# New times for VectorE, GpSimd and row-group visits in the planner that writes a decoder layer's order of issue

## The chip, the core and the metric

The kernel runs on one core of a Trainium2 chip. The core has TensorE (PE in the profile: matrix products into PSUM, eight banks), VectorE (DVE), ScalarE (ACT), GpSimd (POOL) and SyncE (SP, whose queue here starts all transfers). Each engine works through its own list of instructions in order and waits at semaphores for the others. The metric is device time in microseconds, from one launch, lower is better.

## The reference

One post-norm decoder layer on eight sequences of 256 tokens with 256 channels, in float32:

```
x = layernorm(x + attn(x))              # three attentions, 16 heads of 96, mixed by a gate
x = layernorm(x + cross(x, ctx, mask))  # 16 heads of 16 over 256 context tokens
x = layernorm(x + moe(x))               # 8 experts 256->1024->256, all computed, weights of the top 2 router scores
```

The first attention is the sum of three softmaxes with one query: keys from a latent of 32 columns (causal), keys from the 64 tokens with the highest importance score, and plain causal keys. Weights of the expert part: `softmax(one_hot(top2) * scores)`; since the softmax runs over all eight experts, none of them is left out.

## The kernel before, in words

The kernel is written as Python generators ("threads"), one for each kind of work: `project` (queries and keys of a group of four heads), `first` (scores), `weighing` (softmax), `parking` (probabilities are transposed in blocks on VectorE and written to DRAM), `products` (read back from DRAM, probabilities times values), `between` (output projection, first layernorm), `second`, `x_weighing`, `x_products` (cross attention), `after` (second layernorm, router), `experts`, `finish` (third layernorm, store), and loaders. A sequence `s` has four head groups `g`. For the first sequence (`s` = 0) the probabilities are turned by TensorE (`pt`) and copied from PSUM, for the others they go through DRAM (lines 648 to 695).

No loop sets the order in which instructions stand in the engines' lists. A small planner does, `Machine` (from line 131). A thread yields its next operation as an `Op` with a cost in microseconds. `Machine.start` (line 203) works out when it could begin: its engine free, its inputs written, a buffer free. `Machine.run` (line 248) commits, again and again, the operation that could start earliest, and within 0.1 us of it the one of the lowest rank; the rank is a number of the thread's stage and of four times the sequence. So **the costs decide the order**, and the order is all that they decide: no instruction is added or dropped by them, but they also choose the engine where a thread yields a pair. `copied` (line 329) yields VectorE or ScalarE for a copy, `experts` yields either for the ReLU `h`, and `weighing` yields VectorE or GpSimd for one subtraction; the planner takes the one that it believes ends first.

The costs stand in `dve_us` (line 109), `act_us` (line 119), `pool_us` (line 125), in `mm` (line 308: `2 * 0.00084` us for each column, divided by `share` where four products run side by side in TensorE's row or column groups), and in `group` (line 323), which packs several products into one operation and adds `extra` us. Line 100 of the profile is the place where every VectorE, ScalarE and GpSimd instruction is issued, line 315 every product, line 321 every transpose on TensorE, line 306 every transfer: groups are told apart by tile names.

Names that the prediction uses, all as in the profile: `s` are scores of the first attention, with source `kx` for plain and selected keys (probabilities `pr`) and `lx`, `kn` for the latent keys (probabilities `pl`); `o` their product with the values; `pyo` an output projection; `ptx` the transposed, normalised rows; `xpq`, `xq` the cross attention's query; `sx` its scores, `nmx` their negated maxima, `prx` its probabilities, `ox` its products; `pi`, `ppos`, `psel` the choice of the 64 tokens; `plg`, `prt` the router; `ph`, `h`, `py` an expert's two products and the ReLU. "(1,0)" is sequence 1, group 0.

The experts have rank 99: their products (945 of the 1581 us that TensorE is busy) fill whatever the other threads leave open. They need the second layernorm's output of their own sequence, so **there is no filler before the first sequence has passed both attentions**: the first `ph` starts at 236.75 us. PSUM has eight banks for all of this, of which the threads other than `experts` may hold six from then on; SBUF buffers of probabilities are three, shared by `pr`, `pl` and `prx`.

Of the kernel before, what the change touches and what calls it, by code (L numbers as in the profile page):

```python
# [15 lines left out]
PSUM = bass.MemoryType.PSUM  # L16
# [37 lines left out]
def free_size(ap):  # L54
    return math.prod(ap.shape[1:])
# [29 lines left out]
class Issuer:  # L85
# [5 lines left out]
    def __getattr__(self, kind):  # L91
        def make(*args, **kw):
            given = list(args) + list(kw.values())
            aps = [x for x in given if isinstance(x, bass.AP)]
            outs = [kw["out"]] if "out" in kw else [args[0]]
            if kw.get("accum_out") is not None:
                outs.append(kw["accum_out"])
            ins = [x for x in aps if all(x is not y for y in outs)]
            us = self.cost(kind, max(free_size(x) for x in aps), kw)
            return Op(self.name, us, outs, ins, lambda: getattr(self.engine, kind)(*args, **kw), lag=LAG[self.name])  # L100

        return make
# [3 lines left out]
LAG = {"DVE": 0.08, "ACT": 0.1, "POOL": 0.04}  # L106


def dve_us(kind, n, kw):
    if kind == "reciprocal":  # L110
        return 0.06 + 0.0063 * n
    if kind in ("bn_stats", "bn_aggr"):
        return 0.34 if kind == "bn_stats" else 0.1
    if kind in ("match_replace", "max"):
        return 0.42 if n > 8 else 0.2
    return 0.07 + 0.00105 * n + {"scalar_tensor_tensor": 0.06, "tensor_tensor": 0.05}.get(kind, 0.0)


def act_us(kind, n, kw):
    if kind == "copy":  # L120
        return 0.06 + 0.00083 * n
    return 0.16 + 0.00083 * n + (0.1 if kw.get("accum_out") is not None else 0.0)


def pool_us(kind, n, kw):
    if kind == "tensor_tensor":
        return {2: 0.7, 4: 1.0}.get(n, 0.2 + 0.00163 * n)
    return {"tensor_scalar": 0.25 + 0.0025 * n}.get(kind, 0.13 + 0.0009 * n)


class Machine:
# [162 lines left out]
def decoder_layer(ctx: ExitStack, tc: tile.TileContext, a: dict, out: bass.AP):  # L294
    nc = tc.nc
    ctx.enter_context(tc.manual_schedule(engines=ENGINES))
    m = Machine()
    V = Issuer("DVE", nc.vector, dve_us)
    A = Issuer("ACT", nc.scalar, act_us)
    G = Issuer("POOL", nc.gpsimd, pool_us)  # L300

    def dma(out, in_, queue="SP"):
        engine = {"SP": nc.sync, "ACT": nc.scalar}[queue]
        on_chip = out if out.space in ON_CHIP else in_
        size = math.prod(on_chip.shape) * (1 if on_chip.dtype == U8 else 4)
        return Op(queue, 0.6, [out], [in_], lambda: engine.dma_start(out=out, in_=in_), size=size)

    def mm(out, lhsT, rhs, start=True, stop=True, share=1):
        us = 2 * 0.00084 * max(free_size(rhs), free_size(lhsT)) / share
        return Op(  # L310
            "PE",
            us,
            [out],
            [lhsT, rhs],
            lambda: nc.tensor.matmul(out, lhsT, rhs, start=start, stop=stop, skip_group_check=share > 1),  # L315
            lag=0.17,
        )
# [5 lines left out]
    def group(ops, extra=0.0):  # L323
        op = Op("PE", sum(o.us for o in ops) + extra, [], [], lambda: [o.issue() for o in ops], lag=0.17)
        op.writes = list(dict.fromkeys(k for o in ops for k in o.writes))
        op.reads = list(dict.fromkeys(k for o in ops for k in o.reads))
        return op

    def copied(dst, src):

        return V.tensor_copy(dst, src), A.copy(dst, src)
# [13 lines left out]
    def mtile(shape, name):  # L345
        return mtile_(shape, "m", name)
# [9 lines left out]
    def seen(*key):  # L356
        return lambda: (key if len(key) > 1 else key[0]) in done
# [631 lines left out]
    def latent_heads(name):  # L989

        for s in range(B):
            yield 2 + AHEAD * s
            d = pro.setdefault(s, {})
            yield seen("heads", s, 0)
            lk = d["lk"]
            t = (one if name == "kn" else two)([P, NHG, T], name, name)
            ps = [mtile([P, T], "p" + name) for _ in range(NHG)]
            yield m.claim(t)
            yield m.claim(*ps)
            ops = []  # L1000
            for i in range(1 if name == "kn" else 2):
                for g, p_ in enumerate(ps):
                    rows = bass.ts(g, 32)
                    if name == "kn":
                        ops.append((p_, wkv[rows, 0], lk[rows]))
                    else:
                        ops.append((p_[:, bass.ts(i, P)], lk[rows, bass.ts(i, P)], wkv[rows, 1]))
            yield group([mm(*op, share=4) for op in ops], 0.1)
            for g, p_ in enumerate(ps):
                yield copied(t[:, g], p_)  # L1010
                m.release(p_)
            d[name] = t
            done.add((name, s))
            if name != "kn":
                yield seen("kn", s)
                m.release(lk)


    def scores(h, d, g, st, which):


        spans = ((0, N0), (N0, N0 + P)) if which == 0 else ((0, P), (P, T))
        ops = []
        for qt, (lo, n) in enumerate(spans):
            for i in range(3):
                for j in range(HG):
                    rows = bass.ts(j, 32)
                    if which == 0:
                        key = h["kx"][rows, i, 0:n]
                    else:  # L1030
                        key = d["kn"][rows, g, 0:n] if i == 2 else d["lx"][rows, i, 0:n]
                    ops.append(
                        mm(st[j][:, lo : lo + n], h["q"][rows, i, bass.ts(qt, P)], key, i == 0, i == 2, share=4)
                    )
        return group(ops, 0.1)

    def first():
        for s in range(B):
            yield 2 + AHEAD * s
            d = pro.setdefault(s, {})  # L1040
            for g in range(NHG):
                yield seen("heads", s, g)
                h = heads[s, g]
                for which, name in enumerate(("pr", "pl")):
# [6 lines left out]
                    st = [mtile([P, 2 * T], "s") for _ in range(HG)]  # L1051
                    yield m.claim(*st)
                    yield scores(h, d, g, st, which)
                    if which:
                        m.release(h["q"])
# [149 lines left out]
    def kept_in_dram(shape, name):  # L1205
        d = dram.tile(shape, F32, tag=name, name=name)
        Op.kept.add(d.tensor.name)
        return d

    def slots(d, x):  # L1210

        for j in range(HG):
            yield dma(x[bass.ds(32 * j, XH)].rearrange("p g t -> p (g t)"), d.rearrange("(j d i) x -> j d (i x)", j=HG, i=2)[j])
# [62 lines left out]
    def second():  # L1276
        for s in range(B):
            yield 1 + AHEAD * s
            yield seen("middle", s)
            yield seen("query weights")  # L1280
            d, xT, xr = xa.setdefault(s, {}), xTs[s], xrs[s]

            pq = mtile([P, 2, T], "xpq")
            for i in range(2):
                yield group([mm(pq[:, i], xWq[:, k, bass.ts(i, P)], xT[:, k, :], k == 0, k == 1) for k in range(2)])
            qc = one([P, 2, T], "side", "qc")
            for i in range(2):
                yield (
                    A.activation(qc[:, i], pq[:, i], AF.Identity, bias=qb[:, i : i + 1], scale=0.25),
                    V.tensor_scalar(qc[:, i], pq[:, i], 0.25, qb[:, i : i + 1], ALU.mult, ALU.add),  # L1290
                )
            m.release(pq)
            dq = kept_in_dram([P, 2 * T], f"cq{s % 2}")
            yield dma(dq, qc.rearrange("p i t -> p (i t)"))
            m.release(qc)
            yield from slots(dq, xq)
            for i in range(2):
                yield G.tensor_tensor(xr[:, i, :], xr[:, i, :], bo, ALU.add)
            done.add(("bias", s))
            yield seen("context", s)  # L1300
            for g in range(NHG):
                pr = three([P, HG * 2 * T], "p", "prx")
                yield m.claim(pr)
                if g:
                    yield seen("read x", s, g - 1)
                st = [mtile([P, 2, T], "sx") for _ in range(HG)]
                yield m.claim(*st)
                yield group(
                    [
                        mm(st[j][:, qt], xq[bass.ts(j, 32), g, bass.ts(qt, P)], xk[bass.ts(j, 32), g, :], share=4)  # L1310
                        for qt in range(2)
                        for j in range(4)
                    ],
                    0.1,
                )
                d[g] = {"pr": pr, "st": st}
                done.add(("prx", s, g))
# [312 lines left out]
```

## Time and profile before

| what | us |
|---|---|
| three runs: median (lowest, highest) | 1637.23 (1637.2, 1640.49) |
| the profiled execution's own time | 1636.81 |
| its span, first to last instruction | 1635.1 |
| TensorE busy (share of the span) | 1580.7 (97%) |
| VectorE, ScalarE, GpSimd busy | 1101.8 (67%), 592.9 (36%), 612.1 (37%) |
| mean granted TensorE clock | 0.991 |

The profile page has each engine's busy time, the span in 40 slices, the chain that ended last, and the costliest groups of instructions. Other views of the same execution give waits (which engine waited, at which tile, for whom), stretches (busy time and granted clock in a window) and a timeline. TensorE's matmul records overlap, since a product's record covers its pipeline; what a stream of products costs is read from one start to the next.

### The profile page before, as it was taken

The numbers are of one execution on the slowest core, as the hardware profiler recorded it, in microseconds if no ns is written. First come the engines' busy times: TensorE is split into PE (matmuls) and PEld (weight loads), VectorE is DVE, ScalarE is ACT, GpSimd is POOL, SyncE is SP. The second block draws the span as 40 slices with busy tenths as digits, with TensorE's granted clock in tenths as the row PEclk, the third lists the DMA queues.
The fourth block names the chain that finished last, engine by engine and source line by source line (L and its number), as shares of the span: only waits on it lengthen the run. The fifth ranks groups of instructions, "written<-read, shape, count | busy, mean of one in ns | idle before, by whom it ended". The sixth has DMA issues, their size and how long they took to land.

```text
span 1635.1 us, 31737 instructions
## 1 busy us (share of the span) xinstructions
PE 1580.7 (97%) x12028; PEld 1302.6 (80%) x12028; DVE 1101.8 (67%) x2359; ACT 592.9 (36%) x2185; POOL 612.1 (37%) x820
## 2 busy tenths in 40 slices
PE   7889789999999999999999999999999999999998
PEld 6767568887787788788887778878888788888887
DVE  4775687778978755888777854667768683644333
ACT  2564553454453331444355412234435440400000
POOL 4754735354445421444344521334435430310000
PEclk9999899999999999999999999999999999999999
DMA  6511426668766794757658774945747895674553
GB/s 191 152 45 47 164 92 221 198 212 280 230 203 235 236 329 135 273 174 245 206 182 288 253 256 130 325 119 193 246 162 242 276 325 182 219 251 143 160 155 97
DMA packets 185769, 329.95 MB, mean 202 GB/s; under 512 B 13313, under 2 KB 105617, under 8 KB 178449
## 3 DMA queue, kind: packets, MB, share of 16 engines
q1 hardware_dynamic: 185616, 327.92, 60.6%
q8 instruction: 96, 1.57, 0.4%
q14 instruction: 57, 0.46, 0.1%
HBM read 237.70 MB, written 90.19 MB: 201 GB/s over the span
## 4 chain that ended last, share of the span: by engine, by line
PE 74%; issue 7%; DVE 6%; POOL 1%; DMA 1%; ACT 0%; POOLq 0%; DVEq 0%; SPq 0%; ACTq 0%
PE py L315 22%; PE ph L315 22%; PE s L315 7%; PE o L315 3%; PE pk L315 2%; PE pyo L315 2%; PE sx L315 2%; PE ox L315 2%; PE pv L315 1%; PE pkm L315 1%; PE pq L315 1%; PE pks L315 1%; DVE pl L100 1%; DVE pr L100 1%; PE xpq L315 1%
## 5 line engine op out<-in xcount | busy, mean ns | idle before, releaser
L315 PE MATMUL ph<-xT,w 128*128 128x256 f32 x2048 | 476.9, 382 | 0.7 <-DVE turn L100 0.4
L315 PE MATMUL py<-w,h 128*128 128x256 f32 x2048 | 467.8, 381 | 0.0
L315 PEld LDWEIGHTS ph<-xT,w 128*128 128x128 f32 x2048 | 383.0, 190 | 66.3 <-issue 12.1
L315 PEld LDWEIGHTS py<-w,h 128*128 128x128 f32 x2048 | 385.0, 190 | 58.8 <-issue 6.7
L100 DVE TENSOR_SCALAR h<-ph,b 128x256 f32<-128x256 f32 x329 | 158.8, 483 | 133.2 <-PE ph L315 131.3
L100 ACT ACTIVATE h<-ph,b 128x256 f32<-128x256 f32 x183 | 86.6, 473 | 279.5 <-PE ph L315 273.4
L100 DVE SCALAR_TENSOR_TENSOR xr<-py,rw,xr 128x256 f32<-128x256 f32 x128 | 61.5, 480 | 170.5 <-PE py L315 169.6
L100 POOL TENSOR_TENSOR prx<-prx,sumsx 128x512 f32<-128x512 f32 x128 | 129.9, 1046 | 95.5 <-DVE sumsx L100 46.7
L100 POOL TENSOR_TENSOR rstd<-var,nhalf 128x2 f32<-128x2 f32 x24 | 17.3, 722 | 356.7 <-DVE var L100 356.4
L100 ACT ACTIVATE prx<-sx,nmx 128x256 f32<-128x256 f32 x256 | 117.7, 486 | 53.5 <-DVE nmx L100 42.7
L100 POOL TENSOR_TENSOR kx<-turn 128x64 f32<-128x64 f32 (+1 forms) x128 | 65.5, 530 | 178.8 <-DVE turn L100 171.5
L100 POOL TENSOR_TENSOR pr<-pr,wpr 128x256 f32<-128x256 f32 (+2 forms) x128 | 130.5, 1050 | 0.0
L100 ACT ACTIVATE pl<-pl,nmpl 128x128 f32<-128x128 f32 (+1 forms) x256 | 113.6, 448 | 18.9 <-DVE nmpl L100 18.7
L100 ACT ACTIVATE pr<-pr,nmpr 128x128 f32<-128x128 f32 (+1 forms) x256 | 113.7, 447 | 0.0
L100 DVE TENSOR_TENSOR pr<-s,causal 128x256 f32<-128x256 f32 x128 | 74.8, 584 | 38.2 <-PE s L315 34.4
L100 POOL TENSOR_TENSOR pl<-pl,wpl 128x512 f32<-128x512 f32 x64 | 93.0, 1467 | 2.0
L315 PE MATMUL s<-kx,q 32*128 32x192 f32 (+1 forms) x1536 | 92.5, 383 | 0.9 <-POOL kx L100 0.9
L100 POOL TENSOR_TENSOR q<-turn 128x256 f32<-128x256 f32 x64 | 45.5, 728 | 123.3 <-DVE turn L100 123.3
L100 DVE TENSOR_TENSOR pl<-s,causal 128x256 f32<-128x256 f32 x128 | 74.6, 583 | 15.4 <-PE s L315 13.0
L100 DVE TENSOR_REDUCE nmx<-sx 128x2 f32<-128x512 f32 x128 | 79.1, 680 | 7.2 <-PE sx L315 7.2
L315 PEld LDWEIGHTS s<-kx,q 32*128 32x128 f32 x1536 | 68.1, 185 | 18.4 <-issue 6.5
L100 DVE TENSOR_REDUCE nmpr<-pr 128x4 f32<-128x256 f32 (+2 forms) x128 | 80.0, 676 | 0.0
(220 smaller groups left out, 2300.5 us busy)
## 6 DMA issues: line engine op xcount, KB each, us to landing
w<-in_W SPq DMA_DIRECT2D x256, 512.0 KB
pr<-pr SPq DMA_DIRECT2D x28, 1024.0 KB
pa<-pr SPq DMA_DIRECT2D x28, 1024.0 KB
prx<-prx SPq DMA_DIRECT2D x28, 1024.0 KB
xpt<-prx SPq DMA_DIRECT2D x28, 1024.0 KB
pl<-pl SPq DMA_DIRECT2D x28, 768.0 KB
pb<-pl SPq DMA_DIRECT2D x28, 768.0 KB
xT<-in_xT SPq DMA_DIRECT2D x8, 256.0 KB
```

The costliest lines, as they stand in the source:

```text
L100: return Op(self.name, us, outs, ins, lambda: getattr(self.engine, kind)(*args, **kw), lag=LAG[self.name])
L315: lambda: nc.tensor.matmul(out, lhsT, rhs, start=start, stop=stop, skip_group_check=share > 1),
```

## The change

Only the planner's costs change. The functions that make them get a new argument: whether an operand lies in PSUM.

- VectorE: `bn_stats` 0.34 to 0.43 us, `bn_aggr` 0.1 to 0.15; every other operation costs at least 0.11; an operation with `accum_out` (a sum on the side) costs 0.14 more; the additions of 0.06 and 0.05 for `scalar_tensor_tensor` and `tensor_tensor` go, and instead an operation with 256 elements and a PSUM operand costs 0.18 more (`tensor_tensor`) or 0.06 more (`scalar_tensor_tensor`, `tensor_scalar`). Plain copies keep their cost. For the ReLU of 128x256 elements that is 0.339 to 0.399 us on VectorE, beside 0.372 us (unchanged) on ScalarE.
- GpSimd: `tensor_tensor` with 4, 256 and 512 elements 1.0 to 0.87, 0.617 to 0.68 and 1.03 to 1.0 us; `tensor_scalar` by a hundredth or so.
- TensorE: the extra for a visit of row groups (`s`, `sx`, `pkn`, `pvl`) 0.1 to 0.4 us.

```diff
-            us = self.cost(kind, max(free_size(x) for x in aps), kw)
+            us = self.cost(kind, max(free_size(x) for x in aps), kw, any(x.space == PSUM for x in aps))
...
-def dve_us(kind, n, kw):
+def dve_us(kind, n, kw, psum):
     if kind == "reciprocal":
         return 0.06 + 0.0063 * n
     if kind in ("bn_stats", "bn_aggr"):
-        return 0.34 if kind == "bn_stats" else 0.1
-    if kind in ("match_replace", "max"):
-        return 0.42 if n > 8 else 0.2
-    return 0.07 + 0.00105 * n + {"scalar_tensor_tensor": 0.06, "tensor_tensor": 0.05}.get(kind, 0.0)
+        return 0.43 if kind == "bn_stats" else 0.15
+    if kind in ("max", "max_index"):
+        return 0.2
+    us = max(0.07 + 0.00105 * n, 0.11)
+    if kw.get("accum_out") is not None:
+        return us + 0.14
+    if psum and n == 256:
+        return us + {"tensor_tensor": 0.18, "scalar_tensor_tensor": 0.06, "tensor_scalar": 0.06}.get(kind, 0.0)
+    return us
...
     if kind == "tensor_tensor":
-        return {2: 0.7, 4: 1.0}.get(n, 0.2 + 0.00163 * n)
-    return {"tensor_scalar": 0.25 + 0.0025 * n}.get(kind, 0.13 + 0.0009 * n)
+        return {2: 0.7, 4: 0.87, 256: 0.68, 512: 1.0}.get(n, 0.2 + 0.00163 * n)
+    return {"tensor_scalar": 0.26 + 0.0024 * n}.get(kind, 0.13 + 0.0009 * n)
...
-            yield group([mm(*op, share=4) for op in ops], 0.1)
+            yield group([mm(*op, share=4) for op in ops], 0.4)
...
-        return group(ops, 0.1)
+        return group(ops, 0.4)
...
-                    0.1,
+                    0.4,
```

## The prediction

> **What bounds the kernel now.** I read the page's busy times first, then the stretches, then the waits of TensorE before and after 250 us, then the timeline where the longest waits stand.
>
> ```profile
> PE 1580.7 (97%) x12028; PEld 1302.6 (80%) x12028; DVE 1101.8 (67%) x2359; ACT 592.9 (36%) x2185; POOL 612.1 (37%) x820
> ...
> 0.00:50.00 50.00, 39.19 (x307) 32.17 (x308) 26.33 (x76) 14.80 (x46) 25.50 (x57) 1.00 0.66 191
> ...
> 150.00:200.00 50.00, 38.77 (x292) 30.76 (x292) 34.86 (x62) 28.85 (x115) 35.90 (x46) 0.86 0.41 142
> ...
> 250.00:1500.00 1250.00, 1242.17 (x9462) 1021.35 (x9461) 887.18 (x1832) 468.75 (x1744) 462.50 (x602) 1.00 0.68 227
> 1500.00:1600.00 100.00, 100.00 (x465) 88.04 (x464) 35.50 (x77) 0.47 (x1) 0.69 (x1) 1.00 0.50 151
> ```
>
> The columns of a stretch are its length, then busy time and instructions of PE, PE's weight loads, DVE, ACT and POOL, then TensorE's granted clock, DMA share and GB/s. From 250 to 1500 us TensorE idles 7.8 of 1250 us and runs at full clock: its own work is the limit there. In the first 250 us it is busy 210 us (39.2 + 45.3 + 42.1 + 38.8 + 44.9 over the five fifties), idle 40, and the clock falls to 0.86 in one fifty. So a new order can save at most what the start loses, and the few us of waits that come later.
>
> The waits of TensorE up to 250 us (sum, times, longest), and those behind 250 us after the line of dots:
>
> ```profile
> PE pt L321 <- POOL pr L100: 6.3, 5, 1.8
> PE pl L315 <- DMA wA<-in_w_krope: 5.6, 1, 5.6
> PE ppos L315 <- DVE gm L100: 5.5, 3, 2.1
> PE o L315 <- DVE nmx L100: 4.8, 1, 4.8
> PE sx L315 <- ACT prx L100: 4.7, 1, 4.7
> PE ptx L321 <- DVE xr L100: 2.4, 1, 2.4
> ...
> PE prt L321 <- DVE rw L100: 2.1, 1, 2.1
> PE ptx L321 <- DVE xr L100: 1.3, 2, 1.0
> ```
>
> All those of the start sum to 39.8 us, those behind it to 7.6. The two longest stand side by side:
>
> ```profile
> 182.25 2.07 PE L315 MATMUL sx<-xk,xq 32*128 32x256 f32 x10 [4.74 <-ACT prx L100]
> 189.09 1.51 PE L315 MATMUL o<-pa,vw 128*32 128x256 f32 x16 [4.77 <-DVE nmx L100]
> ...
> 181.13 0.23 DVE L100 RECIPROCAL wpr<-wpr 128x16 f32<-128x16 f32 x1
> 186.08 2.31 DVE L100 STREAM_TRANSPOSE pr<-pr 128x2048 f32<-128x2048 f32 x1 [4.71 <-POOL pr L100]
> 188.39 1.83 DVE L100 TENSOR_REDUCE nmx<-sx 128x2 f32<-128x512 f32 x3
> ```
>
> The reader is to see a queue blocked at its head: a transpose of `pr` stands on VectorE right behind the reciprocal that GpSimd's weighting of the same `pr` needs; VectorE idles 4.71 us for GpSimd, and the maxima `nmx` of the next `sx` wait behind it.
>
> **How I count.** No instruction is added or dropped, so I price TensorE's list and compare lists. From start to start in this trace: a product over 256 columns 0.432 us (two records of 0.215; 465 records in 100 us of the end), over 128 columns 0.223, a transpose 0.11, a product in row or column groups a quarter, and 0.1 more at each change between full array and groups (0.309 us instead of 0.216 for the record before it). The order of issue has 321 such changes before and 321 after: TensorE's own work is the same, 1529.7 us by these prices in both lists. What changes is the time lost beside it. I call "loss" the traced start of a group less the prices of all that stands ahead of it. Before: 16.3 us at the first scores, 25.7 at `o` (0,0), 37.0 at (0,3), 39.3 at the first `sx`, 53.5 at `o` (1,0), 62.9 at the first `ph` (236.75 less 173.8), 97.2 at the last `o`. The last 34 us of that come at a rate of 3 us per 100 and are mostly what my prices leave out, as waits are 7.6.
>
> **The change part by part.**
>
> *VectorE's costs.* The masking additions `pr<-s,causal` and `pl<-s,causal` (256 of them) take 0.584 and 0.583 us by their rows; planned 0.389 before, 0.519 after. ReLUs on VectorE take 0.483, planned 0.339, now 0.399. Counting by `accum_out` takes 0.405 (128 columns) and an accumulator read of 0.08; planned 0.204, now 0.344. So the plan's VectorE lagged by about 1.0 us more per head group than it will (8 additions x 0.13), 8 us over the eight groups of the start. Against it: `xr<-pyo` takes 0.420, planned 0.389 and now 0.519. What it does to the list: **17.1 us more of TensorE's work (projections and scores of sequence 1, context products) stand ahead of the first `ph`**, 190.9 us instead of 173.8. That is filler where TensorE waits before the change.
>
> *GpSimd's costs* follow their rows more closely (256 elements 0.73 and 0.62 us, 512 elements 1.046); they move the subtraction `pr<-pr,nmpr` by four from GpSimd (31 to 27) to VectorE, 4 x 0.53 us over the whole run: nothing.
>
> *Row groups, 0.1 to 0.4.* 64 visits `s`, 32 `sx`, 16 `pkn` and `pvl`. In the timeline the 16 records of `sx` take 1.07 us to the next start (planned 0.96, now 1.26), the 24 products of one `s` 2.69 (2.68, now 2.98). The old charge was the nearer one, so this part makes the plan believe TensorE late by some 0.2 x 27 visits = 5 us in the start. A late TensorE in the plan means consumers put too early: it takes back part of the gain.
>
> *Where it lands, step by step.* (1) Up to the first `pt` (0,0) the list is nearly the same, with the same 38.4 us ahead of it; `xpv` now stands ahead of `ppos`, which moves that wait of 1.9 to `pt`. Loss 24.5 there in both: nothing gained. (2) To `o` (0,3). From `s` (kx) to its `pt` the chain needed 28.4 to 31.9 us where `pt` waited; the work in between was 32.4, 27.4 and 22.0 us for groups 1, 2, 3, and is now 27.2, 29.3 and 27.1. Group 3, 8 us short before (the waits of 1.84 and 1.38 on `pr`), is 3 short. With the 24.5 and some 2 of `ppos` the loss at `o` (0,3) becomes about 30 instead of 37: 7 gained. (3) The cross attention's query needs about 7.5 us from `xpq` (ends 153.6) to `xq` (store issued at 154.65, its read 2.56 later, the last of four reads at 158.5 and as long to land; SP's queue held nothing ahead); 7.9 us of work stand there now (16.9 before): no wait, or one of 1. (4) The four `sx`, 1.9, 2.0 and 6.3 us apart before, stand 7.0, 8.9 and 9.8 apart. Eight exponentials take 8 x 0.705 = 5.6 us, so the bank waits of 4.74, 0.76 and 0.53 go. On VectorE 3.7 us of work (`nmpl`, `turn` and others) now stand between that reciprocal and the transpose; but on GpSimd the four weightings of `prx` (4.03 us) have moved in between those of `pr`, so GpSimd needs 0.6 + 2.95 + 4.03 + 1.25 = 8.8 us: VectorE again waits some 5 us, and what queues behind it is the second `nmx`, the copies out of PSUM, and so the third `sx`. I leave 4 us for it, and 3 to 4 for `o` (1,0), whose read-back from DRAM comes 3 us late. (5) `o` (1,1) moves up from 178.2 to 152.9 us of work, with 23.6 us from its `s` (lx) instead of 26.9, where unstalled groups of later sequences had no less than 33.2: it waits, up to 10 us less what (4) already took, some 5. Loss at that point 30 + 2.5 + 8 + 5 = 45 to 47. (6) From there to `ph`, `ox`, `ptx` and `plg` wait as before (6 us; `pyo` to `ptx` has 2.6 us of cover, 2.8 before). Loss at the first `ph` about 53 instead of 62.9: 10 us gained.
>
> *ReLUs move to ScalarE* (329 on VectorE and 183 on ScalarE become 56 and 456). A ReLU takes 0.473 there against 0.483, and both engines have room from 250 us on (ScalarE 469 of 1250 busy, plus 273 x 0.473 = 129): nothing on TensorE's path while PSUM banks come free in time. The tail from 1600 us, `py` to the last store, is the same list: nothing.
>
> **A rule beside the row.** The granted clock was 0.86 between 150 and 200 us, and the 48 `o` products at 189.09 took 3.4 us to the next group, against 1.87 at 131.95; the losses above hold this already. The Trainium skill, "TensorE: Matmul & The Clock Gate", Part 1, says that an idle window of about 3.4 us brings the clock to half. By it, my waits of step 4, each near that length, may or may not cost 1.5 us each again; the sum would be 8 to 11 us instead of 10.
>
> **The sum.** 1635.1 - 10 = 1625.1 us of span, + 1.7 around it (1636.81 less 1635.1) = 1626.8, + 0.4 (the median stands that much above the profiled run): 1627.
>
> **The rivals.**
> - *The chain does not get longer at all* (0.12). First `ph` stays at 236.75; then all 17.1 us are gained: 1620. For it: the waits of the start exceed that. Against: steps 4 and 5.
> - *VectorE paces the start* (0.14). The rows' times of what stands ahead of the second layernorm's `var` on VectorE sum to 186 us against 177; if the start stretches with that, `ph` is at 236.75 x 186/177 = 248.8, 5 us gained: 1632. For it: the blocked queue. Against: VectorE is busy 156 of 235 us there.
> - *Waits only change place* (0.12): the loss stays 62.9, the blocked transpose being paid in full at `sx` and `o` (1,1): 1637.
> - *ScalarE's queue turns into the bound of the middle: slower* (0.25). A ReLU at the head of ScalarE's list waits for its `ph` (279.5 us of idle before 183 of them, 1.5 each), and exponentials stand behind it, so `sx` and `s` banks come free later. 456 x 2.0 us of ReLUs and waits and the 382 us of other work of 250 to 1500 pass 1250. Price: one bank wait like the 4.74; from the third on (14.2 us) it eats the gain and the measurement's bound; one in each of the seven later sequences is 33 - 10 = 23 us slower, 1660. Against it: ReLU waits are there because ScalarE has nothing better, and the planner gives a reader of PSUM the first rank.
>
> **How the numbers follow.** My forecast has 0.37, the two other gains 0.12 and 0.14: faster by over 0.2% (3.3 us, what a measurement here can tell) 0.63; within 0.12; slower 0.25. The range goes from a full gain and 3 us of later waits (1617) to a ScalarE queue that costs four or five such waits (4 x 4.74 - 10 = 9 us, 1645). The likeliest case alone: 1622 to 1631.
>
> **What would show it.** The first `ph` at 240 to 247 us; no wait of `sx` on `prx` near 4.7, but one at `o` (1,0) or (1,1); waits up to 250 us near 30; PE still idle under 10 us from 250 to 1500. It is wrong if TensorE's waits after 250 us exceed 15 us, or the first `ph` comes past 254.

## The result, and the profile after

| | before | after |
|---|---|---|
| median, us (lowest to highest) | 1637.23 (1635.45 to 1644.09) | 1647.99 (1645.06 to 1650.07) |
| ratio, 95% interval | | **1.0059 (1.0042 to 1.0076)** |
| span of the profiled execution, us | 1635.1 | 1645.7 |
| first `ph` starts, us | 236.75 | 262.56 |
| TensorE work ahead of it, by the prices of the prediction, us | 173.8 | 190.9 |
| loss there (start less work), us | 62.9 | 71.7 |

The change made the kernel about 10 us slower, where 10 us of gain were forecast, and its first `ph` came past 254 us, which the prediction had named as a sign that it is wrong. The lines of the page and of the stretches that answer those of before:

```profile
PE 1585.1 (96%) x12028; PEld 1306.3 (79%) x12028; DVE 988.1 (60%) x2070; ACT 722.6 (44%) x2478; POOL 609.1 (37%) x816
...
0.00:50.00 50.00, 37.38 (x290) 30.28 (x294) 25.18 (x71) 13.40 (x36) 23.50 (x56) 1.00 0.75 223
50.00:100.00 50.00, 43.04 (x442) 35.79 (x440) 35.45 (x92) 31.09 (x116) 36.14 (x48) 0.90 0.26 80
...
150.00:200.00 50.00, 43.76 (x329) 35.18 (x327) 36.79 (x68) 25.55 (x101) 33.08 (x43) 0.90 0.35 128
200.00:250.00 50.00, 40.77 (x422) 30.91 (x422) 34.83 (x72) 26.35 (x89) 23.44 (x29) 0.93 0.30 106
250.00:1500.00 1250.00, 1236.37 (x9432) 1016.31 (x9429) 807.71 (x1645) 561.70 (x1970) 464.30 (x604) 1.00 0.66 225
```

ReLUs have gone from VectorE (1101.8 to 988.1 us) to ScalarE (592.9 to 722.6), as planned. In the first 250 us TensorE is busy 210 us, as before: its 40 us of idle time are still 40. From 250 to 1500 us it idles 13.6 us instead of 7.8. TensorE's waits up to 250 us, and those behind 250 us after the dots:

```profile
PE pt L326 <- POOL pr L100: 6.6, 5, 3.4
PE pl L320 <- DMA wA<-in_w_krope: 5.7, 1, 5.7
PE ppos L320 <- DVE gm L100: 5.6, 3, 2.5
PE sx L320 <- ACT q L100: 3.6, 1, 3.6
PE o L320 <- DMA pa<-pr: 3.5, 1, 3.5
PE pks L320 <- DVE pl L100: 2.5, 1, 2.5
...
PE ptx L326 <- DVE xr L100: 4.8, 3, 2.6
PE prt L326 <- DVE rw L100: 4.4, 3, 2.1
```

The wait of `sx` on `prx` (4.74) and that of `o` on `nmx` (4.77) are gone. In their place stand waits at `sx` (3.6), `o` (3.5) and `pks` (2.5), and the sum is 40 us again.

Where the 10.6 us of span arise is seen if the time is read against the work done by then. The table has the time less the prices of all records that TensorE had started (0.1 us per change between full array and groups included; priced by the record, so it lies 2 to 4 us below the losses by the list), in us, for the two kernels and for three that come below:

| up to, us | 100 | 150 | 200 | 237 | 262 | 300 | 1600 |
|---|---|---|---|---|---|---|---|
| before | 25.2 | 35.9 | 53.0 | 61.3 | 62.1 | 64.9 | 97.6 |
| after | 30.0 | 36.8 | 50.0 | 62.4 | 68.3 | 71.9 | 108.4 |
| after, two heads of queue cleared | 28.2 | 35.0 | 49.8 | 56.8 | 64.4 | 65.7 | 99.1 |
| before, VectorE's lag 0.081 | 24.0 | 36.0 | 53.9 | 62.2 | 63.8 | 66.6 | 93.2 |
| before, VectorE's lag 0.082 | 24.4 | 32.4 | 53.8 | 63.1 | 73.1 | 78.2 | 112.8 |

Up to 237 us the two kernels have lost the same. Then the kernel before has its experts' products and stops losing; the kernel after has 17 us of moved work to do first and loses at the old pace, a quarter of a microsecond per microsecond, for 26 us more. So 7.0 of the 10.8 us arise up to 300 us, and 3.8 behind.

Two places of the timeline after show what the moved work does there. The first is around the first `sx`:

```profile
172.17 0.75 POOL L100 TENSOR_TENSOR kx<-turn 128x256 f32<-128x256 f32 x1
172.86 1.42 POOL L100 TENSOR_TENSOR xr<-xr,bo 128x256 f32<-128x256 f32 x2
173.18 2.40 DVE L100 TENSOR_TENSOR pr<-pr,nmpr 128x256 f32<-128x256 f32 x1
...
175.68 0.63 ACT L100 ACTIVATE pr<-pr 128x512 f32<-128x512 f32 x1 [9.49 <-DVE pr L100]
176.62 3.06 PE L320 MATMUL sx<-xk,xq 32*128 32x256 f32 x14 [3.58 <-ACT q L100]
```

A subtraction on VectorE takes 2.40 us here; its shortest takes 0.37. It stands beside GpSimd's additions. ScalarE's queue is blocked at its head by that `pr`, and `sx` waits for a bank that ScalarE has to empty behind it (`q`). The second place is around `o` (1,1):

```profile
211.99 1.51 PE L320 MATMUL o<-pa,vw 128*32 128x256 f32 x16 [3.47 <-DMA pa<-pr]
212.61 0.47 ACT L100 ACTIVATE kc<-xpk,xb 128x256 f32<-128x256 f32 x1 [2.46 <-DMA cv<-vc]
...
215.75 0.20 DVE L100 RECIPROCAL sumsx<-sumsx 128x8 f32<-128x8 f32 x1 [6.05 <-ACT prx L100]
215.87 5.11 DVE L100 TENSOR_TENSOR rows<-lat,ttab 128x128 f32<-128x128 f32 x2
...
215.84 0.98 POOL L100 TENSOR_SCALAR keep<-keep 1x256 f32<-1x256 f32 x1
216.81 4.02 POOL L100 TENSOR_TENSOR prx<-prx,sumsx 128x512 f32<-128x512 f32 x4
```

`kc` and `keep` are keys and their mask for sequence 1's cross attention. `kc` stands at the head of ScalarE's queue, waiting for a buffer whose content is still being stored, with five exponentials `prx` of sequence 0 behind it; GpSimd then does `kc` and `keep` first and weights `prx` at 216.81. At the same time TensorE waits for the read-back of `o` (1,1).

### The profile page after: what moved, and what is told of

Read it like the earlier page. It is cut to its first block, busy times and chain, and to the rows that moved or that the text cites. A ratio compares the mean times of both kernels' runs of the same rounds, so it can differ in the third digit from the quotient of the medians.

```text
span 1645.7 us, 31890 instructions
## 1 busy us (share of the span) xinstructions
PE 1585.1 (96%) x12028; PEld 1306.3 (79%) x12028; DVE 988.1 (60%) x2070; ACT 722.6 (44%) x2478; POOL 609.1 (37%) x816
## 4 chain that ended last, share of the span: by engine, by line
PE 81%; issue 7%; DVE 4%; DMA 4%; POOL 2%; ACT 1%; SPq 1%; POOLq 0%; DVEq 0%; ACTq 0%
PE ph L320 23%; PE py L320 22%; PE s L320 9%; PE o L320 4%; PE pk L320 3%; PE pyo L320 2%; PE sx L320 2%; PE pv L320 2%; PE ox L320 2%; PE pq L320 2%; PE pkm L320 1%; PE pks L320 1%; DMA xpt<-prx 1%; PE pt L326 1%; DVE pr L100 1%
## 5 line engine op out<-in xcount | busy, mean ns | idle before, releaser
L100 ACT ACTIVATE h<-ph,b 128x256 f32<-128x256 f32 x456 | 215.9, 473 | 415.5 <-PE ph L320 414.1
L100 DVE STREAM_TRANSPOSE prx<-prx 128x2048 f32<-128x2048 f32 x28 | 64.5, 2303 | 20.5 <-POOL prx L100 20.5
```

## Experiments

The first theory (**A**) was that the loss lies in the new order up to the second layernorm of sequence 0; its rival, that the ReLUs on ScalarE slow the middle. Letters in the expectations belong to the runs of their own group.

**Start and rest apart.** The planner changes costs when the second layernorm of sequence 0 has been planned.

```diff
+PLAN = {"new": True}                      # e2: False
+    if not PLAN["new"]:
+        return old_dve_us(kind, n, kw)    # likewise POOL and the visits
 ...
             done.add(("normed", s))
+            PLAN["new"] = False           # e2: True
```

New start, old rest:

> The changed costs are used until the first sequence has passed its second layernorm, the old ones from then on; up to the first ph the order of issue is that of the changed kernel. Theory A (the loss is in the start: first ph at 262.6 us with 190.9 us of work ahead, 71.7 lost, against 62.9 before): 8.8 us slower than before, 1646 (1644 to 1648). Theory B (ScalarE's ReLUs slow the middle): 1637 to 1639.

Old start, new rest:

> The old costs until the first sequence has passed its second layernorm, the changed ones from then on. Theory A: the first ph at 236.7 us as before, and what the changed kernel lost after its first ph, 10.7 less 8.8 = 1.9 us: 1639 (1637 to 1641), with most ReLUs on ScalarE. Theory B: 1645 to 1648.

Measured: new start alone 1.0055 (1.0040 to 1.0070), as slow as the whole change; old start with the new rest 1.0014 (1.0003 to 1.0025), 2 us slower, as theory A has it by the ratio (its median of 1642.3 lies between the two ranges; the kernel before had 1639.6 beside it). So the slowdown comes with the new start and not with the ReLUs. This does not say that all of it is made in the start: the rest behind a new start is ordered anew as well.

**The visits apart from the rest.**

```diff
-        return group(ops, 0.1)     # e3, in the kernel before, at its three places
+        return group(ops, 0.4)
-        return group(ops, 0.4)     # e4, in the kernel after
+        return group(ops, 0.1)
```

> Only the charge for a visit of row groups is changed, 0.1 to 0.4. If VectorE's costs made the bad start: 1637, first ph lost time near 63. If the charge made it, since it makes the plan see TensorE late: 1646 to 1648, lost time near 72. If a plan's time is not the sum of its parts: several us away from both, in either direction.

> The change without the charge for visits (0.1 kept). If VectorE's and GpSimd's costs made the bad start: 1646 to 1648. If the charge made it: 1637 or, with the gain that was forecast, 1630. If a plan's time is not the sum of its parts: what this and the run with the charge alone differ from before by does not add up to 10.8.

Measured: visits alone 1.0094 (1.0079 to 1.0109), all the rest without the visits 1.0209 (1.0187 to 1.0232). Alone they cost 15 and 34 us, together 10: the parts do not add up, and none of them is "the" harmful one. Of TensorE's three longest waits up to 260 us with the visits undone, only the first has a like in the kernel after (6.6 us); `o` waits 1.3 us for `pl` there, and `s` never for ScalarE's `kx`:

```profile
PE pt L326 <- POOL pr L100: 9.7, 6, 4.6
PE o L320 <- DMA pb<-pl: 8.1, 1, 8.1
PE s L320 <- ACT kx L100: 6.1, 1, 6.1
```

**One wait of the start at a time.** In the kernel after, GpSimd's one-off fill `xq<-mrow` stands ahead of its weighing of (0,0), and `pt` waits for that:

```profile
58.59 2.80 POOL L100 TENSOR_SCALAR xq<-mrow 128x1024 f32<-128x1024 f32 x1
64.41 0.47 PE L326 MATMUL pt<-ident,pr 128*128 128x128 f32 x1 [3.38 <-POOL pr L100]
```

Here every list is kept and one instruction moves; a table names it by its place in its engine's list.

```diff
+EDITS = [(('POOL', 51), ('POOL', 60), [('POOL', 51)], False)]   # e5, after: behind POOL 60
+EDITS = [(('POOL', 50), ('POOL', 61), [('POOL', 61)], True)]    # e6, before: ahead of POOL 50
-        op.issue()
+        self.put(op)
```

> The kernel after, with one instruction moved: GpSimd's one-off fill xq<-mrow (2.80 us) is issued behind the nine instructions of the weighing of (0,0), as before the change; every other list is that of the kernel after, instruction for instruction. Theory A (the fill held up GpSimd's weighing, and what it cost reached the first ph): the wait of pt on pr falls from 3.4 to under 1.5 us, the clock window at 61.6 (10.24 us at half) to one of 3.41, the first ph comes 3 to 5 us earlier than 262.6, and the time is 1643 to 1645. Theory B (the delay is taken back further on, since the loss at the first sx is 39.9 us against 39.3 before the change): the pt wait falls all the same, but the first ph moves by less than 1.5 us and the time stays at 1647 to 1649.

> The kernel before, with the same single instruction moved the other way: the fill xq<-mrow is issued ahead of the weighing of (0,0), all else as before. Theory A: the first ph comes 3 to 5 us later than 236.75, the time is 1642 to 1644. Theory B: within 1.5 us of the kernel before (1637 to 1640).

Measured: fill late in the kernel after 1.0048 (1.0029 to 1.0066), its first `ph` at 262.84, 0.3 us later than without the move. Fill early in the kernel before 1.0027 (1.0009 to 1.0046), first `ph` at 242.65, 5.9 us later. Not all of the 5.9 is the fill's: read product by product against the kernel before, TensorE is 2.4 us late from behind the fill to 103 us, and the other 3.5 come with a stretch of half clock from 109.7 us and what follows it, which the kernel with the old start shows too, without the fill (last section). So the same step costs some 2.4 us in one order and nothing in the other: theory B for the kernel after, and neither theory's range for the first `ph` of the kernel before. With the fill late, `pt` did wait less, and `pbo`, which needs what GpSimd now does behind the fill, waited instead; TensorE's waits from 20 to 264 us:

```profile
PE pt L355 <- POOL pr L100: 3.8, 3, 1.6
...
PE pbo L349 <- POOL wide L100: 2.1, 1, 2.1
```

**The clock.** In the records of the granted clock, TensorE ran at 0.5 for 27.3 us of the start before and 34.1 after (the last stretch of each reaches past the first `ph`). The next two kernels issue small products ahead of those that wait for data. (Other than the first expectation says, the output is not the same: those ahead of the second `ox` of a pair write over the first 128 columns that the first had summed in one column group. That part of the computation is changed in these two; no instruction of it is missing.)

```diff
+WARM = {42: [(0, 4)], 43: [(0, 10), (1, 5), (3, 2)], 105: [(0, 5)], ...}   # PE's operation: (part, times)
+    def again(out):
+        n = min(free_size(out), P)
+        nc.tensor.matmul(out[:, 0:n], ident[:, : out.shape[0]], ident[:, 0:n], start=True, stop=True, skip_group_check=True)
```

> The kernel after, with 55 small extra products of the identity (128 columns, 0.22 us each) issued ahead of those TensorE instructions of the start that waited for data (ppos, pt, the o of (1,1), ox, ptx, plg), about two thirds of each traced wait; each writes the bank that the next product overwrites, so the output is the same. The granted clock was 0.5 in 34 us of the start after the change, and in 27 us before it; in the windows at 61.6, 211.8 and 259.6 TensorE issued 2.4, 2.5 and 3.0 us worth of work at half speed. Theory C (half of what the start lost is the clock): these windows go or shrink, the first ph comes 4 to 8 us earlier than 262.6, the time is 1640 to 1644. Theory D (the other engines' chains set the start, and a slow TensorE only fills their time): the windows go, but the waits grow by as much, 1646 to 1649. If the extra products come in the way of the real ones: 1650 or more.

> The kernel before with 47 such extra products ahead of its own waits for data (ppos, pt, ox, ptx, plg); its windows of half clock at 62.5, 120.5 and 236.6 held 1.7, 1.8 and 1.7 us of work. Theory C: 3 to 5 us faster than the kernel before (1634 to 1636), which would beat both kernels. Theory D: within 1.5 us of it (1637 to 1640).

Measured: after 1.0035 (1.0018 to 1.0053), first `ph` at 262.73, so nothing gained there; before 0.9983 (0.9966 to 1.0001), first `ph` at 234.12, 2.6 us earlier, short of what C asked for and within what two executions of one and the same start differ by (3.7 us, see the last section). In the kernel after the stretches of half clock at 61.6 and 259.6 went, but those between 175 and 220 us grew from 17.1 to 23.9 us. The work of the program issued at half clock up to the first `ph` is 9.5 us with the extra products and 9.7 without, by the prices. So the run did not take the clock's share away, and it does not decide between C and D.

**The product that waits.**

```diff
+EDITS = [(('PE', 171), ('PE', 178), [('PE', 171), ('ACT', 253)], False)]   # o of (1,1) and its copy
```

> The kernel after, with one product moved: o of (1,1), which waited 3.5 us for its read-back pa and 1.3 us for pb while the queue behind it had work, is issued behind the following pv, xpv and four pt (about 5.3 us of work), its copy oT likewise; all other lists as after. Theory E (the waits of the work that was moved up, each at the head of TensorE's queue, are what the start lost): the wait goes or shrinks to under 1 us, the clock window at 211.8 goes, the first ph comes 3 to 5 us earlier than 262.6, time 1643 to 1645. Theory F (the chain through the other engines sets the first ph, as it did when the fill was moved and when the clock was kept up): the wait goes and the first ph moves by less than 1.5 us, 1647 to 1649.

Measured: 1.0048 (1.0029 to 1.0066), first `ph` at 264.2, 1.6 us later: F, just outside its 1.5. The wait at `o` is gone; one of the transposes that came forward and `plt` behind `o` wait instead. From 172 to 264 us:

```profile
PE plt L355 <- DVE lat L100: 3.2, 1, 3.2
PE pt L355 <- POOL keep L100: 3.1, 1, 3.1
```

**Two heads of queue at once.** By now waits had been cleared or shortened in the kernel after in three ways, each alone, and its first `ph` had not moved by more than 1.6 us. A wait that is cleared alone had uncovered the next; so sequence 1's keys are now put behind on ScalarE, GpSimd and SyncE, alone and together with `o` (1,1). (The entries are set closer here than in the kernel, and the code that moves them is left out.)

```diff
+BEHIND = {
+    ('ACT', 246): ('POOL', 186),  ('ACT', 249): ('POOL', 186),      # kc<-xpk, twice
+    ('POOL', 180): ('POOL', 186), ('POOL', 181): ('POOL', 186), ('POOL', 182): ('POOL', 186),   # keep, kc, keep
+    ('SP', 139): ('POOL', 186),   ('SP', 140): ('POOL', 186),       # their stores
+    ('ACT', 255): ('ACT', 258),   ('SP', 141): ('ACT', 258),        # vc and its store
+    ('PE', 171): ('PE', 178),     ('ACT', 253): ('PE', 178),        # e17 only: o (1,1), oT
+}
```

> The kernel after, with the cross attention's keys of sequence 1, which were planned into the first sequence's cross attention, put behind it: on ScalarE the two kc<-xpk (at the head of its queue at 210.4 for 2.5 us, for the DMA that stores vc, with exponentials prx behind them) go behind the eight prx, on GpSimd keep and kc (2.6 us) go behind the four weightings of prx at 216.8, the stores of both and one copy vc follow; TensorE's and VectorE's lists are as after. Theory L (this head of queue sets the first ph of the kernel after): the exponentials end 2.5 to 3.5 us earlier than 215.5, the weighting of prx starts 5 us earlier than 216.8; as o of (1,1) still waits until 215.6, the first ph gains 0 to 3 us. Theory F (a web of chains: whatever is cleared, the next one stands as long): the first ph within 1.5 us of 262.6.

> The same, and o of (1,1) issued behind pv, xpv and four pt as in the run with the product late. Theory L: with both heads of queue cleared the first ph comes 4 to 7 us earlier than 262.6, time 1641 to 1644. Theory F: the first ph within 1.5 us of 262.6, time 1647 to 1649.

Measured: keys behind 1.0033 (1.0019 to 1.0047), first `ph` at 263.9, so F by the first `ph`; keys and product behind **1.0003 (0.9991 to 1.0016)**, first `ph` at 255.99, 6.6 us earlier. With the keys alone behind, TensorE waited at `o` longer than in the kernel after (4.2 instead of 3.5 us), as the read-back had not moved. With both, the last exponential and the weighting of `prx`, which stood at 215.13 and 216.81, come 5 to 6 us earlier (1.8 of them were there at the first `sx` already, ahead of anything that was moved):

```profile
209.88 0.51 ACT L100 ACTIVATE prx<-sx,nmx 128x256 f32<-128x256 f32 x1
...
210.79 4.48 POOL L100 TENSOR_TENSOR prx<-prx,sumsx 128x512 f32<-128x512 f32 x4 [1.25 <-DMA keep<-in_mask]
```

So theory L holds for the pair: the work of sequence 1 that the new costs moved ahead of the first `ph` held up sequence 0's own chain at two queues in parallel, and both had to be cleared. That gives back 6 us by the medians (1641.9 against 1648.0, not taken side by side), 9 by the ratios, and 4 where both intervals are taken at their near ends (0.26%). The loss at the first `ph` is 65.1 us (255.99 less 190.9), against 71.7 in the kernel after and 62.9 before. `o` (1,1) late without the keys behind is the run above, with nothing gained.

**Nudges that say nothing of the chip.** Does the sign of the change follow from its costs at all? Each kernel below changes one constant of the planner by a tenth of a per cent of a product or by one or two thousandths of a microsecond.

```diff
+        us = 2 * 0.000841 * ...      # e10 before, e12 after (0.00084)
+        us = 2 * 0.000839 * ...      # e15 before
+LAG = {"DVE": 0.081, ...}            # e11 before, e16 after (0.08)
+LAG = {"DVE": 0.082, ...}            # e14 before
```

> The kernel before with TensorE's cost of a column raised by 0.12% in the planner (0.00084 to 0.000841 us), which says nothing new about the chip. The order differs widely; 167.4 us of TensorE work stand ahead of the first ph instead of 173.8. Theory G (the time of a plan scatters by several us with any change of a cost, so that the sign of such a change can't be read from which costs became truer): over 5 us away from the kernel before, in either direction. Theory H (a plan from nearly the same costs is nearly as good): within 3 us of it.

> The kernel before with VectorE's lag raised from 0.080 to 0.081 us in the planner. The first 173.8 us of work up to the first ph are the same in sum, the order differs from about 90 us on. Theory G: over 5 us away from the kernel before; theory H: within 3 us.

> The kernel after with the same 0.12% on TensorE's columns. 170.3 us of work stand ahead of the first ph instead of 190.9. Theory G: over 5 us away from the kernel after (1648), in either direction; theory H: 1645 to 1651.

> The kernel before with VectorE's lag at 0.082 us (0.080 before, 0.081 in the run that was 9 us faster). Theory G (the time of a plan scatters by several us with any change of a cost): anywhere from 1630 to 1655, and not between the other two; theory M (a longer lag of VectorE is nearer the truth and makes the plan better): 1628 to 1634 again.

> The kernel after with VectorE's lag at 0.081 us. Theory M: 5 to 10 us faster than the kernel after, 1638 to 1643. Theory G: no relation to what the same lag did to the kernel before; 1640 to 1660.

> The kernel before with TensorE's cost of a column lowered by 0.12% (0.000839 us; raising it by as much cost 10 us). The work ahead of the first ph is the same 173.8 us, and the order differs in fewer places than with the other nudges. Theory G (scatter): 1630 to 1650, not the mirror image of the raised cost. Theory N (a smooth effect of that cost): about 10 us faster, 1628 to 1632.

| nudge | ratio to the kernel before, 95% interval |
|---|---|
| before, product 0.000841 | 1.0066 (1.0040 to 1.0091) |
| before, product 0.000839 | 0.9963 (0.9947 to 0.9978) |
| before, lag 0.081 | 0.9945 (0.9923 to 0.9967) |
| before, lag 0.082 | 1.0072 (1.0045 to 1.0099) |
| after, product 0.000841 | 1.0048 (1.0031 to 1.0064) |
| after, lag 0.081 | 1.0023 (1.0008 to 1.0039) |

Theory G for the kernel before: it spreads over 21 us between a lag of 0.081 and one of 0.082, and the change's 1.0059 lies inside the spread of nudges that mean nothing. The kernel after moved less: at 0.000841 its 1646.9 us lie in the range of H, at a lag of 0.081 its 1644.9 in that of G. M falls with the lag of 0.082. For the two directions of the product cost the signs are those of N, but one pair does not tell N from G. In the kernels at 0.000841 and 0.082 the first `ph` came early (229 and 227 us), and the loss was made right behind it: 12 and 10 us from 237 to 262 us (the latter in the table above), where the kernel before loses 0.8. Which waits make it was not followed.

The two faster orders gain nothing in the start. Other than the expectation for the lag of 0.081 says, every engine's list is that of the kernel before up to about the first `ph`, for this lag and for 0.000839 alike, and the first `ph` starts at 237.7 in both. What they gain is gained behind it. From 262 to 1600 us TensorE's waits sum to 7.6 us before, 4.3 at 0.000839 and 2.3 at 0.081, all of them here:

```profile
PE ppos L315 <- DVE flag L100: 1.7, 2, 1.3
PE ptx L321 <- DVE xr L100: 0.3, 1, 0.3
PE sx L315 <- DMA xq<-cq: 0.3, 1, 0.3
```

**A version that beats both.** The best order, with small products ahead of its waits for data (none ahead of `ox`):

```diff
-LAG = {"DVE": 0.08, "ACT": 0.1, "POOL": 0.04}
+LAG = {"DVE": 0.081, "ACT": 0.1, "POOL": 0.04}
+WARM = {40: [(0, 5)], 43: [(1, 4), (3, 3)], 87: [(0, 5)], 103: [(0, 5)], 104: [(0, 6), (1, 5), (3, 2)], 195: [(0, 7)], 196: [(0, 2)]}
```

> The order that was 9 us faster than the kernel before (VectorE's lag at 0.081 us) with 44 small extra products ahead of its waits for data (ppos, pt, ptx, plg), without those ahead of ox. Theory C (the extra products keep the clock up and TensorE's own work on the path gets shorter): 2 to 4 us faster than that order, 1627 to 1629, and the fastest kernel of the study. Theory D: as that order, 1630 to 1633.

Measured: 1628.0 us, **0.9932 (0.9913 to 0.9950)** of the kernel before; the same order without the extra products is at 1631.0, and the two intervals overlap. Its stretches:

```profile
50.00:100.00 50.00, 47.53 (x507) 39.17 (x506) 37.15 (x105) 31.90 (x117) 37.17 (x52) 1.00 0.33 103
100.00:150.00 50.00, 46.80 (x483) 39.37 (x482) 29.39 (x80) 21.36 (x69) 25.66 (x34) 1.00 0.11 40
150.00:200.00 50.00, 38.58 (x306) 29.54 (x306) 32.77 (x58) 29.59 (x117) 36.42 (x46) 0.83 0.41 146
```

The granted clock is 1.00 where it was 0.93 and 0.90 with the same order. Only the stretch at 174 us is left, where TensorE waits 4.7 us for a bank and 5.0 for a read-back with no extra product ahead. A stretch at 13 us is missing as well, though no extra product stands near it. That the clock makes the 3 us between the two is not shown.

## Why the prediction was wrong

- **The premise failed: "That is filler where TensorE waits before the change".** The 17.1 us were moved as forecast (190.9 us ahead of the first `ph`), but they did not lessen TensorE's idle time: 40 us of it before, 40 after, and a loss at the first `ph` of 71.7 us where 53 were forecast. I took moved work as TensorE time alone. Each moved head group also puts copies, exponentials, weightings, transposes and transfers into the queues that sequence 0's chain goes through. Clearing two of these gave back 4 to 9 us; that part is shown. The rest of the 10 us has no single cause that these runs found. By the steps below, of the some 19 us of loss too many about 8 arose in step 4, 5 in each of steps 1 and 6, and 3 in step 2.
- **Step 1 failed** ("nothing gained", nothing lost). Up to the first `pt` the list on TensorE is nearly the same, and I looked at no other list. On GpSimd the fill had moved ahead of the weighing: the first `pt` started at 64.41 instead of 59.04, with 38.4 us ahead of it in both. (So the loss at its start was 20.6 us before; the 24.5 that I gave is the loss behind it, at 65.21.) But the fill was not what decided: with it put back the time stayed.
- **Steps 2 and 3** were half right: from the second latent scores to `o` (0,3) the loss grew by 8.1 us instead of 12.1, so 4 of the 7 us came, on top of what step 1 had lost; the query's wait did not come. At the first `sx` both kernels stood level (39.9 against 39.3).
- **Step 4 failed most.** The bank waits on `prx` went, but from the first `sx` to the wait at `o` (1,1) the loss grew by 15.7 us (39.9 to 55.6, which is 59.1 less the wait of 3.47) instead of 8. VectorE's part was mis-sized: 3.58 us came at the first `sx`, by a subtraction of 2.40 us and ScalarE's blocked queue, and `pks` waited 2.5 and 1.9 for VectorE, where I had left 4 us for a VectorE block. The 3 to 4 us at `o` (1,0) did not come. TensorE's work at half clock from 177.7 to 187.9 us adds up to 3.6 (by the prices). Also, "8 x 0.705" adds records that overlap: in the trace before, exponentials `prx` follow each other every 0.45 us, so eight take 3.6 us and not 5.6. **Step 5** was right: `o` (1,1) waited 3.47 and 1.30 us for its read-back, forecast 5.
- **Step 6** failed by 5 us: from `o` (1,1) to the first `ph` I counted the 6 us of waits that stood there before. The loss grew by 12.6 (59.1 to 71.7), of which 1.30 are the second wait of step 5, as other work now stands there.
- **The clock.** In the start's records the granted clock was 0.5 for 34.1 us, before the change for 27.3; by the prices, 11.4 us of work were issued in them instead of 7.5. If such work takes twice its price (the 48 `o` products of the prediction took 3.4 us instead of 1.87), 3.9 us more of the start's loss are TensorE at half speed; this is an estimate, and no run took it away. The prediction named the clock and put it at 0 to 2 us. The window of about 3.4 us that the Trainium skill gives ("TensorE: Matmul & The Clock Gate", Part 1) agrees with the lengths: the stretches last 3.41, 6.83, 10.24 or 13.65 us. That it takes an idle window of that length does not show: the stretch from 62.5 us before follows waits of 1.76, 1.52 and 1.07 us.
- **The rivals.** The slower side came, but not through ScalarE's queue in the middle: the kernel with the new rest alone is 1.0014. "Waits only change place" (1637) was nearest, and its price was too low: in the 26 us by which the start got longer, TensorE lost 6 us more at the old pace (62.4 to 68.3 in the table).
- **What the costs did not give**: the sign. Orders from nudged costs of the kernel before lie from 9 us below it to 12 above, and parts of the change 2 to 34 us above. Of the eleven orders here that came from other costs (the change, four of its parts and six nudges), nine were slower than the kernel before and two faster, so these draws do not bear out even chances either; my range ended at 1645 (its own sum, 4 x 4.74 less 10, gives 1646).

## What to carry to other kernels

Where a greedy planner writes the order, a change of its costs is a new draw from a spread of orders: measure the spread by nudges first, and take the best measured order instead of arguing for the truest cost. Work moved into another engine's idle time is free only if every queue that it passes through is free too; read all five lists, the one-off operations included, before calling it filler. A wait that is cleared alone may only uncover its neighbour, as it did here twice (the fill, the product): clear the heads of two queues together before giving up on a cause.

## What the runs showed of the hardware

- **VectorE held up beside GpSimd for a whole run of instructions.** `rows<-lat,ttab` (128x128, both inputs in SBUF; 0.28 us at its median) took 4.94 us when it started at 216.04: it ended at 220.98, as GpSimd's back-to-back `keep` and four `prx` did (220.83). The same happened in the kernel with the product late. `pr<-pr,nmpr` took 2.40 us instead of 0.37 beside three GpSimd additions, `gate<-gate,gm` 1.67 instead of 0.22 beside two. Summed over VectorE's instructions up to the first `ph`, time above the shortest of the same name and shape is 17.7 us before and 30.7 after, whatever its causes; the planner knows nothing of it. The Trainium skill, "SBUF — State Buffer", "Who interferes with whom", says that a VectorE instruction with two SBUF inputs contends with a GpSimd instruction that reads SBUF, and that the ports they share are an exclusive lock. The trace agrees in that the two end together, in two kernels; here one loser waited through five instructions. That the lock is the cause is the page's reading and was not tested.
- With both heads of queue cleared the two `rows` started ahead of GpSimd's weightings and took 0.45 us together, while `lat` and `rows` behind them took 1.20 and 1.25 beside the weightings, instead of 0.34 and 0.95.
- **The same order does not always get the same clock.** The kernel with the old start has the lists of the kernel before up to about the first `ph`; in its profile the clock was at 0.5 from 107.7 to 111.1 us, in that of the kernel before it was not, `pyo` started at 138.4 instead of 135.2, and the first `ph` at 240.4 instead of 236.75. Differences of that size between two profiles say nothing of their kernels.
